# Slot tables built beside three adjacency sums: two groups in flight, products one turn after their operands, index loads from another queue

## The chip, the cores and the metric

The program runs on one core of a Trainium2 chip. The metric is device time in microseconds. Five engines matter: TensorE (PE in the profile; its weight loads are PEld), VectorE (DVE), ScalarE (ACT), GpSimd (POOL) and SyncE (SP). Each takes its instructions strictly in the order of its own list. DMAs are issued from the lists of SP, ACT and POOL, and an issue can wait there for a semaphore like any other instruction; everything behind it in that list then waits too.

## The reference, cut to what matters

The whole computation is four graph-network layers with a residual layer norm after each: layer 0 (three rounds of an edge network with a segment maximum), layer 1 (three graph convolutions), layer 2 (a relational convolution), layer 3 (a sheaf convolution), on 8192 nodes and 262144 edges sorted by destination. The change lies in layer 1:

```python
def gcn_layer(h, W, b):
    h = h @ W
    msg = norm[:, None] * h[row]
    agg = jax.ops.segment_sum(msg, col, num_segments=N)
    return agg + b
h = jax.nn.relu(gcn_layer(x, W1, b1))
h = jax.nn.relu(gcn_layer(h, W2, b2))
return gcn_layer(h, W3, b3)
```

Here `norm` is the product of the two end nodes' inverse square-root degrees. Layers 2 and 3 aggregate over the same edges, and the kernel prepares tables for them while layer 1 runs.

## The kernel before, in words

Layer 1 has two independent jobs that are woven into each other.

**The sums.** The 8192 x 8192 adjacency counts lie in DRAM as 16-bit floats (`adj`, 134 MB; built during layer 0). A graph convolution is then a dense product. `sum_adj` runs it once per convolution, so there are three passes over all of `adj`. A pass has 16 blocks `d` of 512 destination nodes. A block has four tiles `a` of 2 MB (`q` from 0 to 3), each loaded as two halves of 1 MB (line 1432), one issued from SP and one from ACT. The tile pool has two buffers for `a`. A tile feeds 16 matmuls (line 1442, 512 columns each) whose stationary operand is one 128-node block of the features, split into three bf16 parts: 48 columns in passes 1 and 3 (16 features), 192 columns in pass 2 (64 features), which are cut into 128 and 64, so that pass 2 has 32 matmuls a tile. After four tiles ACT copies the PSUM block out (`ev`, line 1447), and `first`, `second` or `third` (lines 1734 to 1764) finish the block with a few small matmuls and DVE operations. Between two passes `split` (lines 1410 to 1414) cuts the new features into the three parts with three ACT and two DVE operations in a chain; the next pass needs all of it, and the next pass's loads of `a` are issued after it, because its tiles reuse the memory.

**The slots.** `to_slots` (line 1235) is a generator which sorts 64 groups of edges into fixed slots, two groups (one "pair") at a time, 32 pairs in all. For a pair it loads the fields (`ts_f`, line 1241, from SP) and, in two halves of 2304 edges, the group numbers broadcast to the partitions (`ts_oh`, line 1248, one DMA from SP and one from ACT each half). DVE compares them with the partition's number (line 1250), runs a prefix sum (`ts_cum`, line 1252) and multiplies (line 1255); PE turns the result by 18 small matmuls a half into ranks in a PSUM bank `ts_p` (line 1258). ACT copies the ranks out (`ts_r`, line 1262), and some fifteen small DVE operations with two matmuls between them (`ts_ov`, lines 1264 to 1269; `ts_q`, line 1271 and after) place the overflow. Then come six chunks of 12 columns: DVE builds two one-hots and three products (`ts_os` line 1292, `ts_oj` 1295, `ts_v` 1299, two buffers each), and PE does 12 matmuls into `ts_p` (line 1303). ACT copies the finished slots (`ts_e`, line 1307) and SP stores them.

**How they are woven.** `sum_adj` calls `step()` once a tile, ahead of the tile's loads, which advances the generator to its next `yield`. A pair has five yields (two halves, two sets of three chunks, the end), so the 32 pairs take 160 of the 192 steps. A scheduler then puts the instructions of each engine in a list of its own choosing; program order, the dependencies and its estimates set the order, and the hardware follows the lists. Two steps' work can thus stand far from the tile in which it was called.

Of the kernel before, what the change touches and what calls it, by code (L numbers as in the profile page):

```python
# [948 lines left out]
class Sorted(Gnn):  # L949
# [284 lines left out]

    def to_slots(self, sb, ps):

        nc, NB, GC, SJ, CAP = self.nc, self.NB, self.GC, self.SJ, self.CAP
        H, n = GC * P // 2, 2 * GC
        for g in range(0, NB, 2):
            f = sb.tile([P, 2, 5, GC], F16, name="ts_f", bufs=2)  # L1240
            nc.sync.dma_start(f, self.fields[:, g:g + 2])
            a = ps.tile([P, 512], F32, name="ts_p")
            self.clear_bank(a)
            last = 0.0
            for h in range(2):
                oh = sb.tile([P, H], BF16, name="ts_oh", bufs=2)
                for k in range(2):
                    (nc.sync, nc.scalar)[k].dma_start(oh[NB * k:NB * k + NB, :],
                                                      self.ig[g + k, h * H:(h + 1) * H].partition_broadcast(NB))
                nc.vector.tensor_scalar(oh, oh, self.pid64, None, op0=OP.is_equal)  # L1250
                cum = sb.tile([P, H], BF16, name="ts_cum", bufs=2)
                nc.vector.tensor_tensor_scan(cum, self.ones_f[:, 0:1].to_broadcast([P, H]), oh, last,
                                             op0=OP.mult, op1=OP.add)
                last = cum[:, H - 1:H]
                nc.vector.tensor_tensor(oh, oh, cum, op=OP.mult)
                for c in range(GC // 2):
                    o = 2 * (h * GC // 2 + c)
                    nc.tensor.matmul(a[:, o:o + 2], oh[:, c * P:(c + 1) * P], self.which_b, start=False, stop=False,
                                     skip_group_check=True)
                yield  # L1260
            R = sb.tile([P, 2, GC], F32, name="ts_r")
            nc.scalar.activation(R, a[:, 0:n].rearrange("p (c k) -> p k c", k=2), AF.Copy)
            ovi = sb.tile([P, 2, GC], I32, name="ts_ovi")
            nc.vector.tensor_scalar(ovi, R, float(CAP), None, op0=OP.is_gt)
            ov = sb.tile([P, 2, GC], BF16, name="ts_ov")
            nc.vector.tensor_copy(ov, ovi)
            ovf = ov.rearrange("p k c -> p (k c)")
            nc.tensor.matmul(a[:, n:2 * n], self.tri, ovf, start=False, stop=False, skip_group_check=True)
            nc.tensor.matmul(a[:, 2 * n:3 * n], self.ones_b, ovf, start=False, stop=False, skip_group_check=True)
            q = sb.tile([P, n], F32, name="ts_q")  # L1270
            nc.vector.tensor_tensor_scan(q, self.along.rearrange("p k c -> p (k c)"), a[:, 2 * n:3 * n], 0.0,
                                         op0=OP.mult, op1=OP.add)
            nc.vector.tensor_tensor(q, q, a[:, 2 * n:3 * n], op=OP.subtract)
            nc.vector.tensor_tensor(q, q, a[:, n:2 * n], op=OP.add)
            qi = sb.tile([P, 3, n], I32, name="ts_qi")
            nc.vector.tensor_copy(qi[:, 0], q)
            nc.vector.tensor_scalar(qi[:, 1], qi[:, 0], P - 1, None, op0=OP.bitwise_and)
            nc.vector.tensor_scalar(qi[:, 2], qi[:, 0], 7, None, op0=OP.logical_shift_right)
            qf = sb.tile([P, 2, 2, GC], F32, name="ts_qf")
            nc.vector.tensor_copy(qf[:, 0].rearrange("p k c -> p (k c)"), qi[:, 1])  # L1280
            nc.vector.tensor_scalar(qf[:, 1].rearrange("p k c -> p (k c)"), qi[:, 2], float(NB // 2), None, op0=OP.add)
            sj = sb.tile([P, 2, 2, GC], F32, name="ts_sj")
            nc.vector.scalar_tensor_tensor(sj[:, 0], R, -1.0, f[:, :, 3, :], op0=OP.add, op1=OP.add)
            nc.vector.tensor_copy(sj[:, 1], f[:, :, 4, :])
            for k in range(2):
                nc.vector.copy_predicated(sj[:, k], ovi, qf[:, k])
            sh = sb.tile([P, 2, 2, GC], F16, name="ts_sh")
            nc.vector.tensor_copy(sh, sj)
            for k in range(2):
                for c in range(0, GC, 12):  # L1290
                    os_ = sb.tile([P, 12, P], F16, name="ts_os", bufs=2)
                    nc.vector.tensor_tensor(os_, self.row_h[:, None, :P].to_broadcast([P, 12, P]),
                                            sh[:, 0, k, c:c + 12, None].to_broadcast([P, 12, P]), op=OP.is_equal)
                    oj = sb.tile([P, 12, SJ], F16, name="ts_oj", bufs=2)
                    nc.vector.tensor_tensor(oj, self.row_h[:, None, :SJ].to_broadcast([P, 12, SJ]),
                                            sh[:, 1, k, c:c + 12, None].to_broadcast([P, 12, SJ]), op=OP.is_equal)
                    v = sb.tile([P, 12, 3, SJ], F16, name="ts_v", bufs=2)
                    for d in range(3):
                        nc.vector.tensor_tensor(v[:, :, d, :], oj, f[:, k, d, c:c + 12, None].to_broadcast([P, 12, SJ]),
                                                op=OP.mult)  # L1300
                    for j in range(12):
                        o = 3 * n + k * 3 * SJ
                        nc.tensor.matmul(a[:, o:o + 3 * SJ], os_[:, j, :], v[:, j].rearrange("p d s -> p (d s)"),
                                         start=False, stop=False, skip_group_check=True)
                yield
            e = sb.tile([P, 2, 3, SJ], F16, name="ts_e")
            nc.scalar.activation(e.rearrange("p k d s -> p (k d s)"), a[:, 3 * n:3 * n + 6 * SJ], AF.Copy)
            nc.sync.dma_start(self.slots[:, g:g + 2], e)
            yield

    @contextmanager
    def slot_pool(self):
# [104 lines left out]
    def sum_adj(self, t, F, consume, step):  # L1417

        nc, tc, NB, HD = self.nc, self.tc, self.NB, self.HD
        cuts = [(o, min(P, 3 * F - o)) for o in range(0, 3 * F, P)]  # L1420
        with tc.tile_pool(name="sa", bufs=1) as keep:
            s = self.split(keep, t, F, "sp")
            with tc.tile_pool(name="sb", bufs=2) as sb, tc.tile_pool(name="sps", bufs=2, space=PSUM) as ps, \
                    tc.tile_pool(name="sp2", bufs=1, space=PSUM) as ps2:
                for d in range(self.N // 512):
                    out = [ps.tile([w, 512], F32, name=f"s{k}") for k, (o, w) in enumerate(cuts)]
                    for q in range(4):
                        n = 512 // HD
                        step()
                        a = sb.tile([P, n, 16, HD], F16, name="a")  # L1430
                        for h in range(2):
                            (nc.sync, nc.scalar)[h].dma_start(
                                a[:, h * n // 2:(h + 1) * n // 2],
                                self.adj[n * d + h * n // 2:n * d + (h + 1) * n // 2, :, 16 * q:16 * q + 16, :].rearrange(
                                    "h p i f -> p h i f"))
                        for i in range(16):
                            for k, (o, w) in enumerate(cuts):
                                if q == 3 and i == 15:
                                    for j in range(4):
                                        nc.tensor.matmul(out[k][:, j * P:(j + 1) * P], s[:, 4 * d + j, o:o + w],  # L1440
                                                         self.ident_b, start=False, stop=False, skip_group_check=True)
                                nc.tensor.matmul(out[k], s[:, 16 * q + i, o:o + w], a[:, :, i, :],  # L1442
                                                 start=(q == 0 and i == 0), stop=(q == 3 and i == 15))
                    ev = []
                    for k, (o, w) in enumerate(cuts):
                        e = sb.tile([w, 512], F32, name=f"ev{k}")
                        nc.scalar.activation(e, out[k], AF.Copy)
                        ev.append(e)
                    consume(sb, ps2, d, ev)
# [826 lines left out]
```

## Time and profile before

The three timed runs took 16255.13, 16282.36 and 16283.87 us, median 16282.36. The profiled execution took 16247.04 us, and its span is 16245.1 us, so all but 1.9 us lies inside the span.

| part of layer 1 (from the PE and ACT rows of the trace) | from, us | to, us | us |
|---|---|---|---|
| first matmul of pass 1 to its last `ev` | 8564.57 | 9056.77 | 492.2 |
| to the first matmul of pass 2 | 9056.77 | 9194.04 | 137.3 |
| pass 2 to the first matmul of pass 3, with the split between them | 9194.04 | 10028.04 | 834.0 |
| pass 3 to its last `ev` | 10028.04 | 10511.08 | 483.0 |

Layer 1 is thus some 1960 us of the 16245. Over the whole span PE is busy 64%, DVE 66%, ACT 33% and POOL 43%; POOL has nothing at all to do between 8498 and 10562 us. Idle time of an engine in a row is put down to what released the engine, and a row's time before the engine's name is its start and its length. Shares for the whole span say little about this change: layer 1 must be read by its own stretches.

### The profile page before, as it was taken

How to read it: one execution, taken by the hardware profiler on the slowest of the kernel's cores; microseconds unless marked ns; L12 is line 12 of the kernel's file. 1: busy time of each engine (PE TensorE's matmuls, PEld its weight loads, DVE VectorE, ACT ScalarE, POOL GpSimd, SP SyncE). 2: the span in 40 equal slices, each digit the busy share in tenths (PEclk: the TensorE clock that was granted, in tenths of full speed). 3: DMA queues.
4: the chain of work that ended last, by engine and by line, in shares of the span. 5: the costliest groups of instructions: out<-in, count | busy, mean ns of one | idle time of the engine just before them, and what ended most of it. 6: DMA issues, size and time to landing. Idle time of an engine off the chain costs nothing. (4 is left out here: it accounts for less than half of the span.)

```text
span 16245.1 us, 154607 instructions
## 1 busy us (share of the span) xinstructions
PE 10373.5 (64%) x52583; PEld 5085.1 (31%) x52583; DVE 10669.3 (66%) x15323; ACT 5348.3 (33%) x13021; POOL 7015.4 (43%) x7395
## 2 busy tenths in 40 slices
PE   1545545554545454455556698666778878888889
PEld 0222222222222222222223333333332235555544
DVE  7655555445555444555537766399989988888878
ACT  1222222122222212222210000089978825555522
POOL 1777777577777767777760000033222210000051
PEclk7766767666776766677668799777778987888879
DMA  2222222122222222222218456755567753333311
GB/s 72 67 65 70 66 68 67 48 65 70 65 70 69 58 58 65 65 65 71 68 50 285 165 187 211 257 171 180 173 216 248 255 185 125 124 126 124 125 31 27
DMA packets 922515, 1859.22 MB, mean 114 GB/s; under 512 B 402678, under 2 KB 543927, under 8 KB 896886
## 3 DMA queue, kind: packets, MB, share of 16 engines
q1 hardware_dynamic: 522468, 1176.06, 22.2%
q10 hardware_dynamic: 133874, 472.10, 7.9%
q0 software_dynamic: 265376, 201.08, 6.8%
q8 instruction: 422, 6.91, 0.2%
q14 instruction: 375, 3.07, 0.1%
HBM read 1221.16 MB, written 640.32 MB: 115 GB/s over the span
## 5 line engine op out<-in xcount | busy, mean ns | idle before, releaser
L444 POOL DMA_INDIRECT gx<-a_t,ixr x4096 | 3865.7, 944 | 1333.7 <-issue 1213.9
L1609 PE MATMUL t_ps<-ident,gx 128*100 128x128 f32 x1536 | 628.6, 412 | 3551.1 <-DMA gx<-a_t,ixr 2400.2
L444 POOL DMA_INDIRECT gx<-in_x,ixs x2048 | 1932.9, 944 | 624.8 <-issue 606.5
L1384 DVE TENSOR_TENSOR ad_kk<-row_x,oct_k 128x3072 f16<-128x3072 f32 x512 | 1712.4, 3345 | 0.0
L1884 PE MATMUL acc<-tr,hot 128*128 128x392 bf16 (+1 forms) x4608 | 1372.1, 390 | 505.3 <-DVE tr L1870 324.6
L1623 DVE TENSOR_TENSOR_SCAN S<-md,S,p 128x512 f32<-128x512 bf16 x576 | 734.7, 1276 | 1270.0 <-PE p L1620 1269.5
L1609 PEld LDWEIGHTS t_ps<-ident,gx 128*100 128x100 f32 x1536 | 242.4, 158 | 4117.9 <-issue 2109.8
L1442 PE MATMUL s<-a,sp 128*48 128x512 f16 (+2 forms) x4096 | 1278.5, 421 | 270.4 <-DMA a<-adj 270.4
L1617 ACT ACTIVATE h<-p,a_b 128x512 f32<-128x512 f32 x768 | 527.6, 687 | 2549.6 <-PE p L1615 2506.6
L1395 DVE TENSOR_REDUCE ad_n<-ad_st 128x64 f32<-128x1024 f16 x512 | 620.1, 1211 | 1117.7 <-ACT ad_st L1393 1117.7
L444 POOL DMA_INDIRECT xo<-d_t,s_row x256 | 281.1, 1098 | 2421.2 <-DVE d_accs L2099 2245.7
L444 POOL DMA_INDIRECT xo<-c_t,s_row x256 | 303.9, 1187 | 2144.2 <-ACT c_p L1414 2064.1
L1390 PE MATMUL ad_p<-ad_kk,ad_lo 128*128 128x512 f16 x3072 | 1061.0, 485 | 195.6 <-DVE ad_kk L1384 194.0
L1620 PE MATMUL p<-h,a_w 128*128 128x512 f32 x1536 | 1118.2, 820 | 13.6 <-ACT h L1617 5.0
L1393 ACT ACTIVATE ad_st<-ad_p 128x512 f16<-128x512 f32 x1024 | 605.9, 595 | 1477.5 <-PE ad_p L1390 1465.4
L1881 DVE TENSOR_TENSOR tr<-gp,orl 128x384 bf16<-128x384 f32 x2048 | 1035.7, 552 | 65.4 <-PE gp L1935 57.6
L1615 PE MATMUL p<-xt,a_w 100*128 100x512 f32 x1536 | 1048.2, 772 | 7.2 <-ACT h L1617 3.2
L1623 DVE TENSOR_TENSOR_SCAN S<-md,car,p 128x512 f32<-128x512 bf16 x192 | 245.1, 1277 | 1227.2 <-PE p L1620 1227.2
L1935 PE MATMUL gp<-c_p,row 128*64 128x49 bf16 (+1 forms) x8192 | 861.7, 288 | 69.2 <-DVE row L1922 33.4
L1876 DVE TENSOR_TENSOR tr<-gp,orl 128x1568 bf16<-128x1568 f32 x512 | 889.8, 1776 | 2.6 <-PE gp L1935 0.6
L456 ACT ACTIVATE o<-o_ps 128x512 f32<-128x512 f32 x768 | 457.2, 595 | 1314.1 <-PE o_ps L454 1308.8
L1884 PEld LDWEIGHTS <-hot 128*128 128x128 bf16 x4608 | 442.8, 107 | 1063.8 <-issue 978.6
(440 smaller groups left out, 19984.4 us busy)
## 6 DMA issues: line engine op xcount, KB each, us to landing
a<-adj SPq DMA_DIRECT2D x192, 1024.0 KB
a<-adj ACTq DMA_DIRECT2D x192, 1024.0 KB
adj<-ad_st SPq DMA_DIRECT2D x64, 2048.0 KB
md<-m_dst SPq DMA_DIRECT2D x384, 256.0 KB
scan<-o SPq DMA_DIRECT2D x192, 512.0 KB
scan<-o ACTq DMA_DIRECT2D x192, 512.0 KB
dl_hot<-hot ACTq DMA_DIRECT2D x64, 1152.0 KB
hot<-dl_hot SPq DMA_DIRECT2D x64, 1152.0 KB
```

The costliest lines, as they stand in the source:

```text
L444: self.nc.gpsimd.indirect_dma_start(out=out, out_offset=None, in_=table, in_offset=bass.IndirectOffsetOnAxis(ap=ix, axis=0))
L1384: nc.vector.tensor_tensor(kk, self.row_x[:, None, :].to_broadcast([P, 2 * C, 8 * NB]), ok[:, C * g:C * (g + 2), None].to_broadcast([P, 2 * ...
L1390: nc.tensor.matmul(p.rearrange("p i d -> p (i d)"), lo[:, k * C + c, :], kk[:, k * C + c, :], start=(c == 0), stop=(c == C - 1))
L1442: nc.tensor.matmul(out[k], s[:, 16 * q + i, o:o + w], a[:, :, i, :], start=(q == 0 and i == 0), stop=(q == 3 and i == 15))
L1609: nc.tensor.transpose(t.rearrange("r (p k) -> r p k", k=4)[:, :, k], gx[:, a, k].rearrange("p g h f -> p (g h f)"), self.ident)
L1615: nc.tensor.matmul(p1, w1[:, q % 2], xt, start=True, stop=True)
L1620: nc.tensor.matmul(p2, w2, h1, start=True, stop=True)
L1623: nc.vector.tensor_tensor_scan(S[:, k], m[:, k], p2, S[:, q * 512 - 1:q * 512] if q else car, op0=OP.add, op1=OP.max)
L1876: nc.vector.tensor_tensor(tr, gp[:, :, None, :].to_broadcast([P, 4, R, S]), here, op=OP.mult)
L1881: nc.vector.tensor_tensor(tr[:, k], gp, orl[:, q + k, :, None].to_broadcast([P, R, S]), op=OP.mult)
L1884: nc.tensor.matmul(av, hot[:, q + k, :], tr[:, k].rearrange("p r s -> p (r s)"), start=(q + k == 0), stop=(q + k == SJ - 1))
L1935: self.nc.tensor.matmul(out[o], rows[:, j - j0, o], parts[:, 2 * j + h, :], start=True, stop=True)
```

## The change

`slots_of` is now a generator of one pair, and `to_slots` runs several of them: a new one is started every 11 turns, and each turn advances all that live. A pair lives for 13 turns (12 yields and the end), so that two pairs overlap for two turns. The index halves of 2304 become quarters of 1152, with three buffers instead of two. The operands of PE are made in one turn and the matmuls that use them are emitted in the next one: the `yield` stands between the operands and the matmuls, for the ranks (lines 1267 and 1271 of the changed kernel) and for the chunks (its lines 1313 and 1318), where it stood behind the matmuls before. The sets of three chunks become single chunks. Fields and index loads are issued from POOL's queue; both halves of a tile `a` are issued from SP. `step()` is called twice a tile (ahead of the first and of the ninth group of matmuls), after the tile's loads: 384 steps, of which 354 are used.

The core of the diff; the parts of a pair that are only indented anew are left out.

```diff
     def to_slots(self, sb, ps):
+        going = []
+        for g in range(0, self.NB, 2):
+            going.append(self.slots_of(sb, ps, g))
+            for _ in range(11):
+                going = [s for s in going if next(s, self) is not self]
+                yield
+        while going:
+            going = [s for s in going if next(s, self) is not self]
+            yield
+
+    def slots_of(self, sb, ps, g):
-        H, n = GC * P // 2, 2 * GC
-        for g in range(0, NB, 2):
-            nc.sync.dma_start(f, self.fields[:, g:g + 2])
+        H, n = GC * P // 4, 2 * GC
+        nc.gpsimd.dma_start(f, self.fields[:, g:g + 2])
...
-            for h in range(2):
-                oh = sb.tile([P, H], BF16, name="ts_oh", bufs=2)
+        for h in range(4):
+            oh = sb.tile([P, H], BF16, name="ts_oh", bufs=3)
             for k in range(2):
-                    (nc.sync, nc.scalar)[k].dma_start(oh[NB * k:NB * k + NB, :],
-                                                      self.ig[g + k, h * H:(h + 1) * H].partition_broadcast(NB))
+                nc.gpsimd.dma_start(oh[NB * k:NB * k + NB, :],
+                                    self.ig[g + k, h * H:(h + 1) * H].partition_broadcast(NB))
...
             nc.vector.tensor_tensor(oh, oh, cum, op=OP.mult)
-                for c in range(GC // 2):
+            yield
+            for c in range(GC // 4):
                 nc.tensor.matmul(a[:, o:o + 2], oh[:, c * P:(c + 1) * P], self.which_b, ...)
-                yield
         R = sb.tile([P, 2, GC], F32, name="ts_r")
         nc.scalar.activation(R, a[:, 0:n].rearrange("p (c k) -> p k c", k=2), AF.Copy)
+        yield
...
         nc.tensor.matmul(a[:, 2 * n:3 * n], self.ones_b, ovf, ...)
+        yield
...
                 for d in range(3):
                     nc.vector.tensor_tensor(v[:, :, d, :], oj, ...)
+                yield
                 for j in range(12):
                     nc.tensor.matmul(a[:, o:o + 3 * SJ], os_[:, j, :], v[:, j], ...)
-                yield
...
     def sum_adj(self, t, F, consume, step):
                     for q in range(4):
-                        step()
                         a = sb.tile([P, n, 16, HD], F16, name="a")
                         for h in range(2):
-                            (nc.sync, nc.scalar)[h].dma_start(
+                            nc.sync.dma_start(
...
                         for i in range(16):
+                            if i % 8 == 0:
+                                step()
```

## The prediction

> **What bounds the kernel now.** The chain that ended last runs through the end of the program only, so I read layer 1 by stretches first: pass 1, the gap behind it, pass 2, the gap behind that, pass 3 with slot work, pass 3 without.
>
> ```profile
> core 0: us, PE busy (x) PEld busy (x) DVE busy (x) ACT busy (x) POOL busy (x), PEclk, DMA share, GB/s
> 8550.00:9057.00 507.00, 363.78 (x2233) 179.83 (x2233) 376.36 (x515) 15.30 (x35) 0.00 (x0) 0.85 0.82 290
> 9057.00:9194.00 137.00, 33.64 (x370) 28.79 (x366) 136.05 (x179) 13.02 (x11) 0.00 (x0) 0.51 0.18 55
> 9194.00:10003.00 809.00, 808.29 (x3782) 295.57 (x3783) 503.91 (x666) 33.97 (x72) 0.00 (x0) 0.99 0.53 183
> 10028.00:10337.00 309.00, 230.66 (x1406) 115.54 (x1406) 219.42 (x312) 9.41 (x22) 0.00 (x0) 0.87 0.83 294
> 10337.00:10511.00 174.00, 122.05 (x446) 56.20 (x445) 2.70 (x12) 2.96 (x6) 0.00 (x0) 0.75 0.69 266
> ```
>
> Pass 2 is PE's alone (808 of 809 us). Passes 1 and 3 belong to no engine. In the gap of 137 us DVE works without a pause while PE and the DMA stand nearly still: slot work that PE's list had put behind the pass, and ahead of the last blocks' finish and the split, which pass 2 needs. Next, the last five block ends of pass 3, where no slot work is left, and PE between them:
>
> ```profile
> 10388.07 0.59 ACT L1447 ACTIVATE ev<-s 48x512 f32<-48x512 f32 x1 [30.02 <-PE s L1442]
> 10418.84 0.59 ACT L1447 ACTIVATE ev<-s 48x512 f32<-48x512 f32 x1 [30.19 <-PE s L1442]
> ...
> 10511.08 0.59 ACT L1447 ACTIVATE ev<-s 48x512 f32<-48x512 f32 x1 [30.25 <-PE s L1442]
> ...
> 10365.06 8.63 PE L1442 MATMUL s<-a,sp 128*48 128x512 f16 x29
> 10378.25 9.28 PE L1442 MATMUL s<-a,sp 128*48 128x512 f16 x31 [4.55 <-DMA a<-adj]
> ```
>
> A block takes 30.7 us even alone: PE does two tiles in 9.3 us, then waits 4.6 us for the refill of the first, twice a block. Two buffers set this pace, not bandwidth: the DMA is at 0.69. With slot work, pass 1 took 492.2/16 = 30.8 us a block and pass 3 483.0/16 = 30.2. So the slots are free in the passes and cost about 100 us in the gap. The waits of pass 1 (total, times, longest):
>
> ```profile
> PE s L1442 <- DMA a<-adj: 129.9, 46, 7.8
> DVE ts_os L1292 <- PE ts_p L1303: 80.1, 23, 8.9
> DVE ts_q L1271 <- PE ts_p L1269: 38.2, 9, 7.4
> ```
>
> DVE lost 130 us of 507 in all, not one of them for index loads; those cost 185.6 us, all in pass 2, where DVE has time to spare. What a pair costs DVE shows in the gap, from one pair's first small operation to the next one's, with no pause between:
>
> ```profile
> 9078.08 0.19 DVE L1264 TENSOR_SCALAR ts_ovi<-ts_r 128x72 int32<-128x72 f32 x1
> 9117.54 0.19 DVE L1264 TENSOR_SCALAR ts_ovi<-ts_r 128x72 int32<-128x72 f32 x1
> ```
>
> That is 39.46 us with 1.06 us of a block's three finishing operations (lines 1740 to 1742): 38.4 us a pair.
>
> **The change part by part**, against the profiled 16247.0 us (0.2% below the median).
>
> *Start of the layer.* Three scans of 2304 (4.95 us), three compares (0.73 from start to start) and two products (1.27) stand in DVE's list ahead of the split's last operation, 19.6 us; in the changed list three scans, four compares and two products of half the size, about 10.2. The loads now pass through POOL, whose last gather ends at 8498; seven issues stand before the second quarter. Bounds: -9.4 if they are early, 0 if DVE waits for them that long. I take -7, as POOL is free.
>
> *DVE.* Half-size pieces: six more instructions a pair. Below nothing they can't cost; at most 6 x 0.19 us (the smallest row) = 1.1. I take 0.6: 39.0 us a pair. A pass has 128 turns, a pair starts every 11: 11.6 pairs in passes 1 and 2, 8.7 in pass 3, which has slot work for 98 turns, 12.25 blocks. Before, the stores of finished slots count 12 up to the start of pass 2 and 13 and 7 behind that.
>
> *The gap.* In the changed kernel's PE list five chunks and three quarters of ranks (60 and 27 matmuls) stand between the last matmul of pass 1 and the first of pass 2; before it was 19 chunks (228). And in DVE's list the last block's finish stands only about two chunks behind PE's last tile. From that last matmul on: products of one chunk 0.8, `p` 2.0, waiting DVE operations 2, finish 1.0: 6. Then the split's chain: ACT 3.62, DVE 4.42, ACT 3.62, DVE 4.42, ACT 3.62 = 19.7, and slot operations that stand between the two DVE ones (a one-hot, products, a quarter's scan of 2.5, some small), about 5. Loads 9184.35 to first matmul 9194.04: 9.7 as before. Sum 40; were DVE two further chunks late (2 x 3.75), 48. So 137 becomes 40: -97.
>
> *Passes 1 and 3.* DVE needs 39.0 x 8/11 + 1.1 = 29.5 us for a block, and the loads' own pace is 30.7. Neither has slack, so what counts is how much DVE still waits. The list now puts a tile's 16 matmuls in one run and up to 24 products behind them, where PE waited for `a` anyway; operands are a turn old by then, so PE rarely waits for DVE. DVE can run two chunks (7.5 us) ahead of PE's products, and a tile with its wait is 7.7. Bounds for a block: 29.5, DVE without a pause and the loads early; and 39.0, if each pair keeps the 13 us of waits that it had (130 us over 10 pairs): 52.0 x 8/11 + 1.1. The low end is nearer: its own terms, the rank wait (38.2 us) and the products that stood among the S matmuls, are what moves. I take 31.5. Pass 1: 16 x 31.5 = 504 against 492 = +12. Pass 3: 12.25 x 31.5 + 3.75 x 30.7 = 501 against 483 = +18.
>
> *Pass 2.* PE loses 13 - 11.6 pairs; a pair is 72 products (0.76 us for 12), 36 ranks (0.60 for 18) and 0.8 for the rest: 6.6 us. Bounds -9 and 0 (if PE's list only moves); -4. The gap behind pass 2 is a split of 1024 columns with some slot work, as before: 0, with -5 and +5 for the order.
>
> *Queues.* On SP only the loads of `a`, the stores of slots (their wait for `ts_e` on SP was 37.1 us in pass 1) and the small rows remain; the index and field issues that waited ahead of loads (47.7 + 17.8 + 8.7 us in pass 1) go to POOL, behind which nothing is queued until 10562. One queue must now carry both halves. A stretch where SP's queue had the engines to itself, and one with both queues full:
>
> ```profile
> DMA packets 122, 0.51 MB, mean 394 GB/s; under 512 B 0, under 2 KB 0, under 8 KB 121
> q1 hardware_dynamic: 121, 0.50, 95.4%
> ...
> 10373.00:10381.00 8.00, 3.45 (x11) 1.29 (x9) 0.00 (x0) 0.00 (x0) 0.00 (x0) 0.71 1.02 412
> ```
>
> 394 against 412: 0.2 us on a tile of 2.1 MB (5.1 us), and the second issue is 0.37 us later. Bounds 0 and 0.6 us a tile; both are inside my 31.5. POOL issues 9 DMAs a pair; its only direct ones are stores beside a DVE that is 97% busy (1068 of 1100 us from 10600):
>
> ```profile
> L1852 POOL DMA_DIRECT2D lo_cold<-row x128: 531/573/1042, 10573.3 to 11757.8; - x128
> ```
>
> 9 x 0.57 = 5.1 us of the 42 us that a pair lasts: 0, and up to 9.4 us even at the longest row. Cover: three buffers, of which only the last quarter waits for an earlier one.
>
> A rule speaks against this step. The Trainium skill, "SBUF — State Buffer", "Who interferes with whom", says that GpSimd cannot write the descriptors of its DMAs while VectorE holds the shared port pair in a two-port mode, and "A bandwidth-pool intuition that's wrong" on the same page gives about 3.1 us for a DMA that takes 0.62 us alone. By it a pair's nine issues would be an estimated 28 us, still less than a pair, so the sum would stay. The row above shows at most 1.04; this case's trace does not show how much of DVE's work there was of that kind.
>
> **Sum**: -7 - 97 + 12 - 4 + 18 = -78 us. Against the median: 16282.4 - 78 = 16204 us.
>
> **The rivals.** *DVE paces the passes (the other side).* A wait takes the gap's place: PE's list now holds slot and S matmuls in fixed turns, so a late DVE stops PE, and PE stops the loads. With x us a block the passes cost 28.25x + 115.1 - 975.2; against the -108 of the rest this decides from x = 34.3. At 36.5 the passes cost +171 and the time is 16345. For it: 74% was DVE's share of pass 1, and 86% would be needed at 34.3. Against it: DVE's 136 of 137 us in the gap, where nothing but its own products held it. *No cost in the passes*: the loads, freed of the waits on SP, let blocks run at 30: -13, total 16161. For it: single blocks of 26 and 28 us in pass 1. *The gap stays*: DVE is so late at the end of pass 1 that 70 us remain; then -48 in all, 16234. Against it: both lists. *One queue is slower*: at half of 412 GB/s a refill takes 5 us longer, 10 us a block, +282, 16486; the 394 speak against it.
>
> **How the numbers follow.** My forecast has 0.50, no cost in the passes 0.15, the gap stays 0.10, DVE paces 0.21, the queue 0.04. Three timed runs of this kernel differ by 0.18%, so 0.2% or 33 us is about what can be told. The forecast with x from 30.5 to 33 is 16175 to 16246. Faster by over 33 us needs 16250: all of the second, most of the first and third: 0.70. Of DVE's case a third lies within 33 us, and some of the forecast's edge: 0.14; slower 0.16. Range 16135 to 16310: below, x = 29.5 with a gap of 30; above, x = 35.
>
> **What would show it.** Right: under 60 us from the last `ev` of pass 1 to pass 2's first matmul; blocks near 31.5 us; DVE over 90% in passes 1 and 3; no DVE wait for index loads there; POOL issues near 0.6 us. Wrong: PE waiting for `ts_v` or `ts_oh` in passes 1 and 3 by more than 50 us; waits for `a` above the 130 us of before; POOL issues of several us that delay `ts_oh`.

## The result, and the profile after

The changed kernel takes 16183.67 us (median of six runs, 16133.69 to 16195.94) against 16274.28 for the kernel before on the same chip (six runs, 16244.81 to 16288.68). The ratio is 0.9942, 95% interval 0.9926 to 0.9958: 91 us faster, where the prediction on record says 78.

The profiled execution took 16189.75 us, its span is 16188.0. Layer 1, read by the same stretches as before (pass 1, the gap, pass 2, the first ten blocks of pass 3, its last six, of which two still have slot work; columns: stretch, its length, busy time and instructions of PE, PEld, DVE, ACT and POOL, granted clock, DMA share, GB/s):

```profile
core 0: us, PE busy (x) PEld busy (x) DVE busy (x) ACT busy (x) POOL busy (x), PEclk, DMA share, GB/s
8559.00:9061.00 502.00, 375.48 (x2468) 193.62 (x2468) 463.69 (x702) 15.25 (x38) 55.88 (x105) 0.86 0.87 294
9061.00:9100.00 39.00, 8.50 (x100) 6.76 (x99) 39.00 (x51) 11.79 (x5) 3.67 (x7) 0.56 0.28 91
9100.00:9926.00 826.00, 816.42 (x3553) 286.76 (x3553) 427.75 (x617) 31.88 (x66) 46.84 (x89) 0.96 0.52 176
9951.00:10259.00 308.00, 236.04 (x1565) 122.87 (x1563) 290.13 (x439) 9.37 (x23) 30.54 (x57) 0.85 0.87 297
10259.00:10416.00 157.00, 114.47 (x569) 54.48 (x566) 31.49 (x63) 4.24 (x8) 0.00 (x0) 0.91 0.84 312
```

The gap of 137 us is 39. DVE, 74% busy in pass 1 before, is 92% busy there and 94% in the first ten blocks of pass 3. Pass 2 is still PE's, but at a clock of 0.96 instead of 0.99. Between the same events as in the table of before:

| part of layer 1 | before, us | after, us | difference | predicted |
|---|---|---|---|---|
| start of pass 1 | at 8564.57 | at 8559.48 | -5.1 | -7 |
| pass 1 | 492.2 | 501.6 | +9.4 | +12 |
| gap | 137.3 | 38.6 | -98.7 | -97 |
| pass 2 and the split behind it | 834.0 | 850.9 | +16.9 | -4 |
| pass 3 | 483.0 | 465.8 | -17.2 | +18 |

That is -94.7 us in the end of the layer. (What follows layer 1 took 5734 us in the profile of before and 5772 in this one; it spreads from 5722 to 5772 over the first ten kernels told of here, whose code there is the same. So single executions can differ by tens of microseconds behind the layer; the 91 us rests on the medians, the stretches on one profiled execution of each kernel.)

The waits of pass 1 in the changed kernel (total, times, longest):

```profile
PE ts_p L1271 <- DVE ts_oh L1267: 43.9, 24, 6.6
PE ts_p L1318 <- DVE ts_v L1313: 42.3, 24, 3.9
PE s L1456 <- DMA a<-adj: 31.6, 16, 5.3
...
DVE ts_os L1306 <- PE ts_p L1318: 20.0, 9, 3.7
DVE ts_oh L1262 <- DMA ts_oh<-ig: 14.7, 7, 3.4
```

The direction has turned round. Before, PE waited 129.9 us for `a` and DVE 80.1 + 38.2 us for PE's slot matmuls; now PE waits 42.3 us for `ts_v` and 43.9 for `ts_oh`, and DVE hardly waits. PE's idle time in pass 1 stays about the same: 129.3 us of 492.2 before, 126.4 of 501.6 after. The index loads issue from POOL at the price that was foreseen (min, median, longest, in ns):

```profile
L1260 POOL DMA_DIRECT2D ts_oh<-ig x256: 516/523/783, 8523.7 to 10229.6; - x128
```

### The profile page after: what moved, and what is told of

It is laid out like the page before. It is cut to its first block, busy times and chain, and to the rows that moved or that the text cites. A ratio compares the mean times of both kernels' runs of the same rounds, so it can differ in the third digit from the quotient of the medians.

```text
span 16188.0 us, 154932 instructions
## 1 busy us (share of the span) xinstructions
PE 10394.0 (64%) x52583; PEld 5088.7 (31%) x52583; DVE 10686.3 (66%) x15515; ACT 5348.6 (33%) x13021; POOL 7170.9 (44%) x7683
## 5 line engine op out<-in xcount | busy, mean ns | idle before, releaser
L1479 ACT ACTIVATE away<-row_f,s_dl 128x128 bf16<-128x128 f32 x2304 | 739.6, 387 | 0.3 <-issue 0.2
```

## The experiments

Three theories stood at the start. A: the gain comes from issuing both halves of `a` on SP, because it changes what the scheduler puts where. B: it comes from the generators (stagger, late products, two turns a tile). C: it comes from POOL's index loads. Two later ones, D and E, parted A: D, the order of PE's list makes the gap; E, loads issued from ACT stand behind ACT's own waits on the chip. "Chunk" is one set of 12 columns, 12 products in PE's list; how many stand where was counted in each kernel's list.

All runs in one table; the stretches are those of the table above, with the split on its own. "Layer" is from the first matmul of pass 1 to the last `ev` of pass 3.

| kernel | median, us | ratio to before, 95% | pass 1 | gap | pass 2 | split | pass 3 | layer |
|---|---|---|---|---|---|---|---|---|
| before | 16274 | 1 | 492.2 | 137.3 | 808.0 | 26.0 | 483.0 | 1946.5 |
| changed | 16184 | 0.9926 to 0.9958 | 501.6 | 38.6 | 826.8 | 24.1 | 465.8 | 1856.9 |
| before, `a` from SP alone | 16234 | 0.9951 to 0.9977 | 530.8 | 48.6 | 827.6 | 22.3 | 481.5 | 1910.8 |
| changed, `a` from SP and ACT | 16308 | 1.0008 to 1.0026 | 532.7 | 116.1 | 799.7 | 25.5 | 511.9 | 1985.8 |
| changed, no index loads from POOL | 16197 | 0.9935 to 0.9961 | 513.9 | 32.7 | 811.5 | 21.9 | 498.4 | 1878.4 |
| changed, products in the same turn | 16199 | 0.9932 to 0.9957 | 502.2 | 37.4 | 821.2 | 21.1 | 478.9 | 1860.8 |
| changed, no POOL loads, `a` from SP and POOL | 16273 | 0.9998 to 1.0015 | 494.5 | 120.1 | 812.8 | 25.6 | 506.3 | 1959.4 |
| changed, 4/12/6 turns | 16219 | 0.9961 to 0.9980 | 479.0 | 38.3 | 837.2 | 23.8 | 483.0 | 1861.2 |
| changed, three buffers for `a` | 16130 | 0.9909 to 0.9934 | 488.7 | 39.4 | 805.9 | 24.7 | 437.4 | 1796.1 |
| both of these | 16122 | 0.9900 to 0.9926 | 446.5 | 37.9 | 838.0 | 21.5 | 442.7 | 1786.6 |
| changed, pairs one by one | 17766 | 0.9922 to 0.9951 | 504.8 | 37.8 | 801.0 | 23.4 | 489.9 | 1856.9 |
| changed, ranks in halves | 17739 | 0.9906 to 0.9943 | 490.5 | 40.0 | 819.1 | 22.8 | 466.8 | 1839.1 |
| 4/12/6, three buffers, four `ts_oh` | 17638 | 0.9845 to 0.9882 | 401.9 | 33.8 | 828.8 | 22.5 | 425.5 | 1712.5 |
| the same, four chunk buffers | 17617 | 0.9835 to 0.9871 | 404.6 | 33.4 | 834.7 | 24.0 | 419.7 | 1716.4 |

Each row's stretches come from one profiled execution, and how far a stretch varies from one execution to the next no run here shows; so a difference of some 10 us in one stretch alone is not taken for shown. The last four ran later, beside a kernel before that took 17863 us then, and their ratios are to that time; their layer 1 starts at 10006 to 10043 us instead of about 8560, for a reason that is open. No trace of the kernel before is from then: that layer 1 itself had its usual length is inferred from "pairs one by one" and "ranks in halves" (1856.9 and 1839.1 us beside 1856.9).

**One part alone: both halves of `a` from SP, in the kernel before.**

```
-                            (nc.sync, nc.scalar)[h].dma_start(
+                            nc.sync.dma_start(
                                 a[:, h * n // 2:(h + 1) * n // 2],
```

> The kernel before with one edit: both halves of every tile of `a` are issued from SP. Everything else of the slot work is as before (halves of 2304 indices, index loads from SP and ACT, products in the turn of their operands). PE's list then holds 36 products and 72 ranks between pass 1 and pass 2, where the kernel before holds 228 and 126. Theory A (the loads make the gain): the gap behind pass 1 is 35 to 45 us instead of 137; pass 1 takes up slot work that the gap had and goes to about 32.5 us a block (520); pass 3 has slot work for 8 blocks at 33 and 8 blocks at 26.5 without (476); pass 2 as before (834): -73 us, near 16200, a ratio of 0.9955. Theory B (the generators make it: stagger, late products, two turns a tile): the gap stays above 100 us, and only the blocks without slot work gain, 4 to 8 x 4.2 us: about 16245, 0.998. Theory C (POOL's index loads make it): as B.

Measured: 16233.79 us against 16278.87, ratio 0.9964. Pass 1 and the gap:

```profile
8571.93:9102.69 530.76, 379.33 (x2540) 192.37 (x2540) 487.67 (x670) 15.62 (x39) 0.00 (x0) 0.87 0.81 278
9102.69:9151.34 48.65, 7.71 (x120) 6.19 (x120) 48.58 (x44) 12.14 (x7) 0.00 (x0) 0.53 0.30 94
```

The gap goes without any change to the generator: B and C fall for the gap. Pass 1 pays for it, 531 us with DVE 92% busy, since PE's list now holds 75 chunks there where it held 54. This edit alone is worth 45 us, half of the gain. A expected 73: the measured time lies nearer to B's 16245 than to A's 16200, and it is the gap that decides between them.

**The other parts alone: the changed kernel with `a` from SP and ACT again.** The same edit backwards.

> The changed kernel with one edit undone: the second half of every tile of `a` is issued from ACT again. The generators and POOL's index loads stay. PE's list then holds 204 products and 108 ranks between pass 1 and pass 2 (60 and 27 in the changed kernel). Theory A (the loads make the gain): the gap is back at 110 to 130 us, blocks without slot work are back at 30.7 us, pass 1 is 480 to 490: 480 + 120 + 845 + 490 against the 1857 us of the changed kernel is about +75 us, near 16260, no faster than before. Theory B (the generators): the gap stays near 40, and only the blocks without slot work lose, about 5 x 4.2 = 21 us: near 16205. Theory C (POOL): as B.

Measured: 16308.41 us, ratio 1.0017: the generators and POOL's loads, without the change of queue, make the kernel slower. The gap is 116 us. Pass 1 was worse than A had it, 533 us instead of 480 to 490:

```profile
PE s L1456 <- DMA a<-adj: 149.3, 42, 9.2
...
DVE ts_os L1306 <- PE ts_p L1318: 113.7, 29, 9.5
```

PE waits for `a` and DVE waits for PE, as in the kernel before. So the parts do not add: -45 for the queue alone, +30 for the rest alone, -91 for both.

**Two queues, but not ACT's.** From the kernel with index loads on SP and ACT (the next experiment), the second half of `a` goes to POOL.

```
-                            nc.sync.dma_start(
+                            (nc.sync, nc.gpsimd)[h].dma_start(
                                 a[:, h * n // 2:(h + 1) * n // 2],
```

> The changed kernel with index loads from SP and ACT and fields from SP (as in the run where POOL issues none of them), and the second half of every tile of `a` issued from POOL, whose list holds nothing else in layer 1. So each tile has two queues again, but neither is ACT's. PE's list holds 180 products and 108 ranks between pass 1 and pass 2 (72 and 9 with both halves on SP). It parts two effects of the second queue. Theory D (the list): the pile behind pass 1 comes from how the scheduler reckons with two queues, so the gap is back at 100 to 120 us although no load can stand behind ACT's work, near 16260 to 16290. Theory E (ACT's list): loads issued from ACT come late behind `ev`, `ts_r` and `ts_e`, and that makes the pile on the chip, so the gap is 30 to 50 us, near 16200. Both: blocks of pass 3 without slot work take 26.5 us if ACT's list was what made them 30.7; 30.7 if two queues as such do.

Measured: 16272.90 us, ratio 1.0007. The gap and its neighbour:

```profile
8559.23:9053.68 494.45, 367.93 (x2174) 178.78 (x2175) 354.23 (x533) 13.85 (x32) 43.54 (x62) 0.85 0.82 290
9053.68:9173.83 120.15, 27.81 (x300) 23.26 (x300) 118.70 (x173) 12.71 (x9) 1.42 (x2) 0.51 0.18 62
```

The gap is back although POOL's list holds nothing else that could hold a load up: D holds, E falls. Six kernels fall into two groups by the products that PE's list holds behind pass 1: 228, 204 and 180 with two queues went with gaps of 137, 116 and 120 us; 36, 60 and 72 with one queue with 49, 39 and 33. Why the scheduler delays slot work when `a` has two queues was not tried; that it reckons with tiles twice as early is a guess. The blocks without slot work could not be read, because slot work reached the end of pass 3 here.

**POOL's index loads undone.**

```
-        nc.gpsimd.dma_start(f, self.fields[:, g:g + 2])
+        nc.sync.dma_start(f, self.fields[:, g:g + 2])
-                nc.gpsimd.dma_start(oh[NB * k:NB * k + NB, :],
+                (nc.sync, nc.scalar)[k].dma_start(oh[NB * k:NB * k + NB, :],
```

> The changed kernel with the index loads issued from SP and ACT in turn and the fields from SP, as before; POOL issues nothing in layer 1. `a` stays on SP alone, the generators stay. PE's list holds 72 products and 9 ranks between pass 1 and pass 2. Theories A and B: index issues stand in SP's list ahead of loads of `a` and wait for `ts_oh` there, some 75 us in a pass before, of which little reached PE: within 20 us of the changed kernel, 16180 to 16205. Theory C (POOL's index loads make the gain): 60 us or more of the gain is lost, 16240 or above, with PE's waits for `a` in pass 1 back above 100 us.

Measured: 16197.15 us, 13 us above the changed kernel with overlapping intervals. C falls. In the layer it costs 21 us, 33 of them in pass 3, and pass 2 gives 15 back.

**The lateness undone.** The `yield` ahead of the 9 ranks and of the 12 products moves behind them.

```
             nc.vector.tensor_tensor(oh, oh, cum, op=OP.mult)
-            yield
             for c in range(GC // 4):
                 ...
+            yield
```

> The changed kernel with the products and ranks written in the turn of their operands (each turn's end stands behind the matmuls instead of ahead of them). The planner gives PE's list 60 products and 27 ranks between pass 1 and pass 2, as many as in the changed kernel, and about the same number of chunks in each block. Theory A: the late products are worth little, since the planner places them by its own times: 16175 to 16200, and PE's waits for `ts_v` and `ts_oh` in pass 1 stay near 92 us. Theory B: the lateness saves waits, so without it PE waits for `ts_v` and `ts_oh` well above 92 us in pass 1, blocks go from 31.4 to 33 or more, and the time is 16230 or above.

Measured: 16199.06 us, 15 us above the changed kernel, again inside the intervals; the layer is 4 us longer. PE's waits in pass 1 are 42.8 us for `ts_oh` and 40.5 for `ts_v`, as with late products. The scheduler places them by itself, and the written turn hardly counts.

**The stagger undone.**

```
-            going.append(self.slots_of(sb, ps, g))
-            for _ in range(11):
-                going = [s for s in going if next(s, self) is not self]
-                yield
+            yield from self.slots_of(sb, ps, g)
```

> The changed kernel without the stagger: the pairs' generators run one after the other, 12 turns each, so that no two pairs are under way at once in the order of the program. PE's list holds 70 products and 27 ranks between pass 1 and pass 2 (60 and 27 in the changed kernel) and slot work up to block 14 of pass 3 (12). If the stagger is worth little: pass 1 near 500 us, two or three more blocks of pass 3 at 30 instead of 26.5 us, +10 to +15: 16190 to 16205. If the stagger is what the generators bring when both halves of `a` come from SP: DVE pauses inside each pair (for `ts_r` and the first products, some 11 us), pass 1 goes to 530 and the time to about 16235, as with the loads on SP alone.

Measured: ratio 0.9937, layer 1856.9 us, the same as with stagger: worth nothing that can be told.

**Two halves instead of four quarters.**

```
-        H, n = GC * P // 4, 2 * GC
+        H, n = GC * P // 2, 2 * GC
-        for h in range(4):
-            oh = sb.tile([P, H], BF16, name="ts_oh", bufs=3)
+        for h in range(2):
+            oh = sb.tile([P, H], BF16, name="ts_oh", bufs=2)
```

> The changed kernel with the ranks in two halves of 2304 indices instead of four quarters of 1152 (two `ts_oh` buffers). PE's list holds 48 products and 36 ranks between pass 1 and pass 2. If the size of the pieces matters: a half costs DVE some 7 us (0.73 + 4.95 + 1.27) ahead of its ranks instead of 3.8, so PE's waits for `ts_oh` in pass 1 grow from 44 to 65 us or more, and the time is 16210 or above. If it does not: 16170 to 16195.

Measured: ratio 0.9925, layer 1839.1 us; PE waits 45.7 us for `ts_oh` in pass 1, no more than with quarters. The quarters bring nothing that can be told. So none of the generator's parts, undone by itself, loses what the generators gain beside a single queue (1910.8 to 1856.9 us in the layer). What the runs leave over is how thickly the slot work lies (160 of 192 turns, 75 chunks in pass 1, against 354 of 384 turns and 67 chunks), the single chunks in place of sets of three, the turns behind a tile's loads instead of ahead of them, and several parts together. None of these was tried, so where this second half of the gain comes from is open.

**What paces pass 1: fewer turns there.** 4, 12 and 6 turns a block in the three passes instead of 8.

```
-                            if i % 8 == 0:
+                            if (16 * q + i) * turns % 64 < turns:
                                 step()
```

> The changed kernel with 4 turns a block in pass 1, 12 in pass 2 and 6 in pass 3 instead of 8 everywhere. Pass 1 then has 44 chunks instead of 64 in PE's list, pass 2 about 95 instead of 71, pass 3 53 as before. Theory A with DVE as the pace of pass 1 in the changed kernel: DVE needs 7.3 x 39 + 18 = 303 us there, so the loads' own 26.5 us a block set the pace: pass 1 about 435 (501.6 in the changed kernel), pass 2 +26 for four more pairs of PE's work, pass 3 456 (465.8): about -50 us, near 16133. Rival (the loads or PE's list set the pace of pass 1, and DVE is busy beside them): pass 1 stays near 31 us a block, and pass 2's +26 makes it slower than the changed kernel, near 16205.

Measured: 16219.25 us, near the rival's number. (The lists hold 48 and 67 chunks in pass 1; 44 and 64 was miscounted.) Pass 1 has a third less DVE work (318 us busy in 479, 464 in 502 before the edit) and takes 29.9 us a block all the same. DVE's waits there:

```profile
DVE v L1754 <- PE p L1752: 75.7, 6, 24.6
DVE ts_oh L1262 <- DMA ts_oh<-ig: 46.8, 6, 23.5
```

So DVE's throughput is not the whole of the pace.

**Three buffers for `a`.**

```
-                        a = sb.tile([P, n, 16, HD], F16, name="a")
+                        a = sb.tile([P, n, 16, HD], F16, name="a", bufs=3)
```

> The changed kernel with three buffers for `a` instead of two, nothing else. Theory A with DVE as the pace: pass 1 loses at most the waits for `a` (31.6 us) and stops at DVE's 29.5 us a block, 475 to 490; blocks of pass 3 with slot work about 29.5; only the five blocks without slot work become much shorter, 21 us for four tiles of 5.1 us instead of 26.5: -15 -8 -27 = -50 us, near 16135. Rival (the refill of two buffers sets the pace of passes 1 and 3, and DVE is busy beside it): blocks of 24 to 26 us with slot work too, -150 us, near 16035. If the buffers do not matter at all: 16184.

Measured: 16129.91 us, near theory A's 16135, but not by its terms alone: pass 1 gained 13 us for 15 and pass 3 28 for 35, and pass 2, where no gain was expected, is 21 us shorter (805.9 for 826.8, at a granted clock of 0.98 for 0.96). Waits of pass 1, then pass 1 and the end of pass 3 by stretches:

```profile
PE ts_p L1318 <- DVE ts_v L1313: 66.0, 36, 8.3
...
PE s L1456 <- DMA a<-adj: 0.7, 1, 0.7
```

```profile
8559.08:9047.75 488.67, 367.70 (x2464) 193.43 (x2462) 463.27 (x699) 15.26 (x38) 55.92 (x105) 0.87 0.89 301
...
10250.00:10355.00 105.00, 82.14 (x417) 40.15 (x416) 11.12 (x24) 2.71 (x5) 0.00 (x0) 0.98 0.95 376
```

With 8 turns a block, taking the waits for `a` away only moves them to `ts_v`: pass 1 gains 13 us and DVE is at 95%. Without slot work a block falls to 20.5 us, the loads' own pace at 376 GB/s.

**Both edits.**

> Both: 4, 12 and 6 turns a block and three buffers for `a`. Theory A: pass 1 is free of DVE and of the refill and runs at the loads' 5.1 us a tile, 22 to 23 us a block: about 365 (-137); pass 2 +26; pass 3 433 (13 blocks at 27.8 to 29, three at 21: -33): -144 us, near 16040, a ratio of 0.9855 to the kernel before, and more than the sum of the two edits alone (-100). Rival (something else holds pass 1 at 26 us or more, the DMA's bandwidth beside other transfers): the sum of the two, near 16085.

Measured: 16121.94 us, inside the intervals of three buffers alone; pass 1 446 us instead of 365. That is 27.9 us a block, as the rival had it (26 or more, though it named the DMA's bandwidth), but the time is above the rival's 16085 as well. The blocks of pass 1 lie between 18 and 41 us, and the four longest hold one thing (DVE's wait in total, times and longest; then timelines of POOL, DVE and PE; start, duration, in brackets the wait before):

```profile
DVE ts_oh L1262 <- DMA ts_oh<-ig: 62.2, 7, 20.0
...
8805.08 3.10 POOL L1260 DMA_DIRECT2D ts_oh<-ig x6 [21.57 <-PE ts_p L1271]
...
8813.88 0.52 DVE L1262 TENSOR_SCALAR ts_oh<-ts_oh,pid 128x1152 bf16<-128x1152 bf16 x1 [19.97 <-DMA ts_oh<-ig]
...
8818.18 0.40 PE L1271 MATMUL ts_p<-which_b,ts_oh 128*128 128x2 bf16 x9 [8.46 <-DVE ts_oh L1267]
```

POOL's issue of a pair's fourth quarter waited for ranks of an earlier quarter, which free one of the three `ts_oh` buffers; DVE lay idle 20 us until the load had landed; then PE waited 8.5 us for DVE, and with PE the loads of `a`: SP issued none between 8810.15 and 8826.67.

**A fourth `ts_oh` buffer.**

```
-            oh = sb.tile([P, H], BF16, name="ts_oh", bufs=3)
+            oh = sb.tile([P, H], BF16, name="ts_oh", bufs=4)
```

> 4, 12 and 6 turns a block, three buffers for `a`, and four buffers for `ts_oh` instead of three. In the run with three, DVE waits 62.2 us for index loads in pass 1 (7 times, up to 20), because the fourth quarter's load waits on POOL's queue until PE has done ranks of an earlier quarter, and PE then waits up to 8.8 us for `ts_oh` (34.4 in all). If this ring holds pass 1 up: both waits fall below 20 us, pass 1 from 446 to about 415, the time from 16122 to about 16095. If not: within 10 us of 16122.

Measured: ratio 0.9863, layer 1712.5 us instead of 1786.6. Waits of pass 1:

```profile
PE ts_p L1271 <- DVE ts_oh L1267: 7.0, 3, 3.7
...
DVE ts_oh L1262 <- DMA ts_oh<-ig: 3.4, 1, 3.4
```

Index waits go from 62.2 to 3.4 us, PE's from 34.4 to 7.0, pass 1 from 446 to 402 (415 expected). The ring made these waits. The scheduler's list moved with it (36 products and 45 ranks behind pass 1 instead of 0 and 72), so how much of the 74 us in the layer is the ring's alone is not shown.

**Four buffers for `ts_os`, `ts_oj` and `ts_v` too** (`bufs=2` to `bufs=4` in their three lines).

> As the run with four `ts_oh` buffers, and four instead of two buffers for `ts_os`, `ts_oj` and `ts_v`, so that DVE can run four chunks ahead of PE's products. If DVE's pace binds only where chunks stand densely in PE's list (six in a block take DVE 22 us, beside 21 us of loads): PE's waits for `ts_v` in pass 1 fall from 51.5 to about 25, another -25 us: near 16070. If DVE's list lets it run ahead no further than before: within 10 us of the run with four `ts_oh` buffers.

Measured: ratio 0.9853, layer 1716.4 us. PE's waits for `ts_v` in pass 1 are 43.1 us (41.8 without): the depth changes nothing there, and the step in the ratio lies inside the intervals. Either version beats both kernels, by 1.4 to 1.5% against before.

## Why the prediction was right or wrong

**The gap: right, to 2 us.** 137 to 40 was forecast from the lists, and 38.6 was measured, with its terms: from the last `ev` to the split 5.7 us for 6, the split with the slot operations in it 22.6 for 24.7, from its end to the first matmul 10.3 for 9.7. What the prediction did not say is which edit shortened the list. It credits the change as a whole; the runs show that it is the queue of `a` alone, the edit that it costed at 0 to 0.6 us a tile.

**Pass 1: right in size, +9.4 for +12.** 31.35 us a block against 31.5. That neither DVE nor the loads have slack is what the runs show: with three buffers for `a` the block stays at 30.5 while DVE is busy 95%; with a third less DVE work it stays at 29.9; only with both edits does it fall, to 27.9, and with the fourth `ts_oh` buffer to 25.1. But the step "PE rarely waits for DVE" was wrong: 86 us of such waits in pass 1. The prediction named more than 50 us of them as a sign of being wrong, and that sign came. The time was right all the same because these waits took the place of waits for `a`, which fell from 130 to 32 us.

**Pass 3: wrong, -17 for +18.** PE's list has slot products in twelve blocks, as reckoned (12.25). The first ten came out at 30.9 us (31.5 in the sum). Two terms failed. The one price for every block with slot work was too high for the last two, which hold chunks but no ranks any more: 24.6 and 25.6 us, 13 us less than in the sum. And the 30.7 us of a block without slot work, taken as the pace that two buffers set, was the pace of two buffers behind two queues: the last four blocks average 26.7, 16 us less in all. Two blocks' ends and PE between them, at the end of the changed kernel's pass 3:

```profile
10309.57 0.59 ACT L1461 ACTIVATE ev<-s 48x512 f32<-48x512 f32 x1 [18.46 <-PE s L1456]
10337.07 0.59 ACT L1461 ACTIVATE ev<-s 48x512 f32<-48x512 f32 x1 [26.91 <-PE s L1456]
...
10318.41 9.06 PE L1456 MATMUL s<-a,sp 128*48 128x512 f16 x32 [3.57 <-DMA a<-adj]
10331.43 5.11 PE L1456 MATMUL s<-a,sp 128*48 128x512 f16 x15 [3.95 <-DMA a<-adj]
```

With SP alone in the kernel before, where that is the only edit, the last blocks lie between 24.8 and 27.8 us too, so the queue does it. Three of their ends:

```profile
10431.28 0.59 ACT L1447 ACTIVATE ev<-s 48x512 f32<-48x512 f32 x1 [26.82 <-PE s L1442]
10456.03 0.59 ACT L1447 ACTIVATE ev<-s 48x512 f32<-48x512 f32 x1 [24.16 <-PE s L1442]
10482.73 0.59 ACT L1447 ACTIVATE ev<-s 48x512 f32<-48x512 f32 x1 [26.12 <-PE s L1442]
```

Over the last four blocks, PE's waits for `a` fell from 9.4 to 7.2 us a block (37.6 and 28.8 in all), and PE's own time from 21.4 to 18.7 us, at a granted clock of 0.74 before and 0.89 after; so only about half of the gain is a shorter wait, and whether the clock rose because PE waits less is not shown. The prediction looked for the price of one queue in bandwidth (394 against 412 GB/s) and found a loss of 0.2 us a tile; measured it was a gain of about 1 us a tile. Why PE waits less for tiles from one queue is open: in the last blocks of the kernel before, the two halves were issued within 0.17 us of each other, so ACT was not late. The Trainium skill, "DMA: Bandwidth & Descriptors", "Issuing engines are not separate DMA queues", says that several issuing engines share the same 16 DMA engines and save issue time only; the trace agrees that the second queue bought no bandwidth (266 GB/s over the last four blocks before, 295 after), and shows it as a loss.

**Pass 2: wrong, +17 for -4.** PE did lose slot work as reckoned: 11 chunks of products, 8 us. The term that the sum put at nothing is the granted clock: 0.99 in pass 2 before, 0.96 after. The rows of the two S matmuls over 660 us of pass 2, first the changed kernel, then the kernel before (count, busy, mean ns):

```profile
L1456 PE MATMUL s<-a,sp 128*64 128x512 f16 x800 | 333.9, 417 | 0.0
L1456 PE MATMUL s<-a,sp 128*128 128x512 f16 x799 | 321.1, 402 | 2.5 <-DMA a<-adj 2.5
```

```profile
L1442 PE MATMUL s<-a,sp 128*64 128x512 f16 x834 | 338.4, 406 | 0.0
L1442 PE MATMUL s<-a,sp 128*128 128x512 f16 x834 | 327.0, 392 | 0.7 <-DMA a<-adj 0.7
```

10 ns on each of 2048 matmuls are 21 us; PE's waits inside pass 2 add 8 (13.7 against 5.9), and less slot work takes about 10 off. The traces' clock records put 65 us of pass 2 at half clock in the changed kernel and 22 in the kernel before; the mean of these matmuls goes with that time: 408 ns with 65 us, 400 with 22, and 397 with 7 in the changed kernel with `a` from SP and ACT. Pass 2 varies from 800 to 827 us over the kernels with 8 turns a block, so the term is no fixed price of the change, and what sets it is open.

**Start, DVE, POOL: right.** -5.1 us for -7. DVE's busy time in the layer rose from 1248.9 to 1271.0 us, 0.7 us a pair for 0.6. POOL's issues of index loads have a median of 0.523 us and a longest of 0.783, beside a DVE that is 92% busy: the blocked issue that the prediction weighed is in no row of this layer. DVE's waits for index loads in pass 1 were not nil, but 14.7 us.

**The rivals.** "DVE paces the passes" was right in part, below its deciding point: PE now waits for DVE, but a block takes 31.35 and 30.9 us, not 34.3. "One queue is slower" had the sign wrong. That the sum came out close is luck in so far as its two large misses, +21 us in pass 2 and -35 in pass 3, have opposite signs; the -97 of the gap, which carries it, was no luck.

## What to carry to other kernels

Where a scheduler writes the engines' lists, the queue a load is issued from is an input to that order: compare the lists, and count what stands between the last matmul of one stage and the first of the next, before costing any edit. A busy engine paces a stage only as long as nothing else holds it: cutting DVE's work by a third gained under 5% of pass 1 (501.6 to 479.0 us); a third buffer for `a` then gave 33 us, and a fourth for a ring whose release hung on another engine 45 more. Take an isolated stretch's pace as the pace of its whole set-up, queues included, and not of the one resource that comes to mind.

## What was not expected of the hardware

The granted clock falls inside pass 2, also where PE has no pause at all. Ten microseconds in the changed kernel behind a block's end, and what PE did up to there:

```profile
9250.00:9260.00 10.00, 10.00 (x36) 3.13 (x35) 5.13 (x7) 0.00 (x0) 0.00 (x0) 0.66 0.23 95
```

```profile
9245.52 1.07 PE L1760 MATMUL p<-ev,b_w 128*64 128x512 f32 x2
9246.52 1.07 PE L1761 MATMUL p<-ev,b_w 64*64 64x512 f32 x2
9247.52 1.07 PE L1764 MATMUL p<-row,b_b 1*64 1x512 f32 x2
9248.52 0.76 PE L1318 MATMUL ts_p<-ts_v,ts_os 128*128 128x108 f16 x12
9249.33 1.18 PE L1769 MATMUL p<-b_w,h 64*128 64x16 f32 x8
```

Here 4 us of the block's small matmuls and slot products stand in one run, and the clock of the next 10 us is 0.66. Two other falls looked at (at 9404 and 9616 us) come behind such runs as well. In all the clock's records hold twelve falls in this pass, ten of them behind the end of a block and two behind a pause of PE, and four in the kernel before, all behind block ends; both kernels have sixteen such ends, so the run alone does not decide. The Trainium skill, "TensorE: Matmul & The Clock Gate", "What's actually happening", ties the clock to how busy PE has been over windows of about 3.4 us and halves it after an idle one; these rows agree if a run of small matmuls counts as idle, which no run here isolates. If so, the place of small matmuls in a dense stage would be a cost of its own.
